# The first upsampling of the MLP: TensorE reads its operand with columns outside

## The chip, the cores and the metric

The kernel runs on one core of a Trainium2 chip, as one program in one launch. The metric is device time in microseconds (us). Three executions before the change took 17002.19, 17007.7 and 17019.74 us; their median is 17007.7 us. The profile is of a further execution.

## The reference, cut to what matters

Eight images of 48 x 48 points with 96 channels pass through four layers, each added to its input behind a group normalisation (`_gn`). Layers 0, 2 and 3 are selective scans and hold nearly all of the work. Layer 1, the MLP, is where the change lies: the normalised image is upsampled along both sides by a band-limited filter, goes through two dense maps with a quadratic between them, and is filtered back to 48 x 48.

```python
x = x + _L0_conv_ref(_gn(x), ...)     # scan in four directions
xc = jnp.transpose(x, (0, 3, 1, 2))   # layer 1
xu = _upsample_rfft(xc)               # height and width
h = jnp.transpose(xu, (0, 2, 3, 1))
h = h @ W1.T + b1
h = coef[:, 0] + coef[:, 1] * h + coef[:, 2] * (h * h)
h = h @ W2.T + b2
hl = _lpf_rfft(jnp.transpose(h, (0, 3, 1, 2)), cutoff=0.5)
out = hl[:, :, ::2, ::2]              # added to x
x = x + _L2_conv_ref(_gn(x), ...)     # scan along lines
x = x + _L3_conv_ref(_gn(x), ...)     # scan in four directions
```

The filters are linear, so the kernel applies each as a matrix: `upt` (48 x 73) takes 48 points to 73, and `downt` (73 x 48) takes them back. An upsampling along the height is thus one matrix product with the height on the partitions.

## The kernel before, in words

**Stages.** The program has three stages one behind another: `ss2d("l0")` (layer 0), `lines` (layer 2) and `ss2d("l3")` (layer 3). Each walks over 8 images, 4 directions and 5 blocks of up to 10 lines of 48 points, 160 blocks in all. A block takes four turns, so a stage has 640 turns and an image 80. A turn is one pass of the loop in `scans`: three scans on VectorE (L337, 128 x 968 values each), the exponentials that feed them on ScalarE (`make_da`, L329, six a turn, written to PSUM tile `ps_da`, which has two buffers), the products that feed them on VectorE and GpSimd (`make_dbu`, L305), the products behind them on GpSimd (`make_hc`, L343) and the sums over states on TensorE (`reduce`, L363 and L365). VectorE waits for `ps_da`; ScalarE in turn waits for the scan that frees a buffer of it.

**The guest.** Layer 1 has no stage of its own. A class `Guest` hands out its steps one by one between the turns' instructions, during the stages `l0` and `lines`, image by image as layer 0 finishes them. Stage `l3` has the same code as `l0` and no guest. The order of every engine's instructions is the order in which the program is written; no scheduler reorders them. `aside`, called twice a turn (for slots `at` and `at + 1`), first calls `guest.settle()`, which issues what had been left behind (the ScalarE half of a step), and last `guest.turn()`, which issues new steps: for a step of kind "psum" the matmul at once, into a free PSUM bank (`side` or `s1` in `l0`, shown as `ps_side` and `ps_s`; `sa` or `sb` in `lines`), and its ScalarE half at the next `settle`, one half turn later. The exponentials of the following half turn are queued on ScalarE right behind what `settle` issued.

**The first upsampling.** For each image, 24 channels at a time are loaded as `xt`, height on the 48 partitions, then channel, then width (L1130). `heighten` (L1144) is called three times for each such load, with 8 channels each: a TensorE matmul of `upt` with 8 channels x 48 columns of `xt` (384 columns in all, L1145) and a ScalarE copy from PSUM into `xh` (L1147), which is laid out as 73 rows of height on partitions, then width, then 24 channels. Both `xt` and `xh` are parts of one tile, `g_room` in the profile. When three copies are done, `keep` (L1160) sends `xh` to memory as `upd`. Before the change the matmul's output runs channel by channel, and the copy turns the order: it reads PSUM straight on and writes each next value 24 values (96 bytes) on. There are 8 x 4 x 3 = 96 such matmuls and 96 such copies in the program. In the profile each matmul of 32-bit values stands as two records, so L1145 has 192.

**Other lines that the steps touch.** `done` in `ss2d` (L762) is a ScalarE copy from PSUM into an image laid out by lines; in two of the four directions it writes by columns, so that each next value is 48 values (192 bytes) on, in the other two straight on. `s0` in `ss2d` (L721) is a TensorE matmul whose moving operand is that same kind of view: straight on in two directions, 192 bytes a step in the two others. The four directions follow each other for each image in the order straight, column, column, straight. `raw` (L711) is a TensorE matmul into bank `s1`, whose result ScalarE reads at L715.

The helper that the copy used before splits a row of PSUM into runs of 48:

```python
def rows(t, n):
    return t[:, :n].rearrange("p (r s) -> p r s", s=SEG)   # SEG = 48
```

Of the kernel before, what the change touches and what calls it, by code (L numbers as in the profile page):

```python
# [15 lines left out]
H, W, C = 48, 48, 96  # L16
# [20 lines left out]
UG = 73  # L37
# [3 lines left out]
HS = 8  # L41
# [21 lines left out]
def rows(t, n):  # L63

    return t[:, :n].rearrange("p (r s) -> p r s", s=SEG)
# [37 lines left out]
def vss_stack_kernel(ctx: ExitStack, tc: tile.TileContext, i: dict, out: bass.AP):  # L103
    nc = tc.nc
# [890 lines left out]
    class Guest:  # L995
# [54 lines left out]
        def items(self):  # L1050
# [4 lines left out]
            upt, downt = self.tile([H, UG], "upt"), self.tile([UG, H], "downt")  # L1055
# [4 lines left out]
            def part(at, rows_, *shape):  # L1060
                n = int(np.prod(shape))
                v = room[:rows_, at:at + n]
                return v.rearrange("p (a b) -> p a b", b=shape[1]) if len(shape) == 2 else v
# [34 lines left out]
            xt, xh = part(0, H, HC, W), part(HC * W, UG, W, HC)  # L1098
# [6 lines left out]
            for b in range(nb):  # L1105
# [36 lines left out]
                       lambda p: nc.scalar.activation(bl, p[:C, :1], AF.Identity, bias=bias))  # L1142

                def heighten(s0):  # L1144
                    return ("psum", lambda p: nc.tensor.matmul(p[:UG, :HS * W], lhsT=upt, rhs=xt[:, s0:s0 + HS, :],  # L1145
                                                               start=True, stop=True),
                            lambda p: nc.scalar.copy(xh[:, :, s0:s0 + HS].rearrange("p w c -> p c w"),  # L1147
                                                     rows(p[:UG], HS * W)))

                for c0 in range(0, C, HC):  # L1150
                    for s0 in range(0, HC, HS):
                        yield heighten(s0)
                    yield "wait", 1
                    if c0 + HC < C:
                        yield "do", lambda: load_xt(c0 + HC)
                    yield "wait", 1

                    def keep():
                        for s in UCUT:
                            nc.sync.dma_start(upd[s, :, c0:c0 + HC], xh[s])  # L1160
                    yield "do", keep
                    yield "wait", 2
# [194 lines left out]
```

## Time and profile before

| | |
|---|---|
| median of three executions | 17007.7 us |
| the profiled execution | 17010.73 us |
| its span, first to last instruction | 17007.9 us |
| mean granted clock of TensorE | 0.854 |
| first scan of `l0`, of `lines`, of `l3` | 103.8, 5844.3, 11616.4 us |
| L337 scans, 5760 | 11822.8 us busy, mean 2075 ns |
| L329 exponentials, 11520 | 7419.0 us busy, mean 649 ns |
| L343 products on GpSimd, 3840 | 10065.4 us busy, mean 2635 ns |
| L1145 matmul records of the first upsampling, 192 | 482 ns the shortest, 915 ns the longest |
| L1147 copies of the first upsampling, 96 | 1092 ns the shortest, 1239 ns the longest |

The first copy starts at 1101.4 us and the last at 8788.6 us, so 72 of the 96 stand in `l0` and 24 in `lines`. "Busy" is the time in which at least one instruction of a group runs; on ScalarE an instruction's record can reach into the next one's, so that the distance between two starts is shorter than the duration. In a windows view, a row gives for a stretch of the span the busy time of each engine with its count of records, the granted clock of TensorE as a share of full speed (PEclk), and what the DMA engines did.

### The profile page before, as it was taken

How to read it: one execution, taken by the hardware profiler on the slowest of the kernel's cores; microseconds unless marked ns; L12 is line 12 of the kernel's file. 1: busy time of each engine (PE TensorE's matmuls, PEld its weight loads, DVE VectorE, ACT ScalarE, POOL GpSimd, SP SyncE). 2: the span in 40 equal slices, each digit the busy share in tenths (PEclk: the TensorE clock that was granted, in tenths of full speed). 3: DMA queues.
4: the chain of work that ended last, by engine and by line, in shares of the span. 5: the costliest groups of instructions: out<-in, count | busy, mean ns of one | idle time of the engine just before them, and what ended most of it. 6: DMA issues, size and time to landing. Idle time of an engine off the chain costs nothing.

```text
span 17007.9 us, 172189 instructions
## 1 busy us (share of the span) xinstructions
PE 13000.3 (76%) x53740; PEld 4643.6 (27%) x53740; DVE 15774.2 (93%) x9680; ACT 13824.5 (81%) x20812; POOL 15185.0 (89%) x7999
## 2 busy tenths in 40 slices
PE   6778887888787777777777777776777777777776
PEld 1223232333332333233323332221222222222221
DVE  7999999999999799999999999997999999999998
ACT  6878878888787688888888888886877878878876
POOL 7998989998889788888888888887999999999998
PEclk7878888889898789889989998887888878878887
DMA  4555555564555444544454444444545455555554
GB/s 149 180 170 172 180 163 182 171 185 169 173 172 179 141 153 167 167 161 164 158 171 159 158 166 160 160 156 139 180 168 181 173 170 176 176 172 176 175 176 143
DMA packets 931143, 2844.03 MB, mean 167 GB/s; under 512 B 396668, under 2 KB 464988, under 8 KB 803406
## 3 DMA queue, kind: packets, MB, share of 16 engines
q1 hardware_dynamic: 930222, 2833.03, 49.9%
q8 instruction: 422, 6.91, 0.2%
q14 instruction: 499, 4.09, 0.1%
HBM read 2384.40 MB, written 448.17 MB: 167 GB/s over the span
## 4 chain that ended last, share of the span: by engine, by line
POOL 24%; DVE 22%; ACT 21%; issue 18%; PE 10%; DMA 3%; SPq 1%; POOLq 0%; DVEq 0%; ACTq 0%
DVE dbu L337 15%; POOL dbu L343 14%; ACT ps_da L329 8%; POOL dbu L305 7%; DVE dbu L305 6%; ACT L329 3%; POOL dds L507 3%; PE ps_y L363 2%; ACT ps_b L286 1%; DMA bc<-bcd 1%; DMA dd<-dds 1%; PE ps_side L582 1%; PE ps_s L711 1%; ACT L739 1%; PE ps_sb L874 1%
## 5 line engine op out<-in xcount | busy, mean ns | idle before, releaser
L337 DVE TENSOR_TENSOR_SCAN dbu<-ps_da,dbu 128x968 f32<-128x968 f32 (+3 forms) x5760 | 11822.8, 2075 | 782.2 <-ACT ps_da L329 644.7
L343 POOL TENSOR_TENSOR dbu<-dbu,bc 128x1440 f32<-128x1440 f32 (+1 forms) x3840 | 10065.4, 2635 | 1486.5 <-DVE dbu L337 948.7
L329 ACT ACTIVATE ps_da<-dd,w_l_a 128x484 f32<-128x484 f32 (+3 forms) x11520 | 7419.0, 649 | 2395.5 <-DVE dbu L337 2166.1
L363 PE MATMUL ps_y<-dbu,w_red 128*32 128x480 f32 (+1 forms) x23040 | 4282.5, 658 | 1806.8 <-POOL dbu L343 1744.4
L365 PE MATMUL ps_y<-dbu,w_red 128*32 128x480 f32 (+1 forms) x7680 | 4242.3, 658 | 0.0
L305 DVE TENSOR_TENSOR dbu<-dd,ps_b 128x962 f32<-128x962 f32 (+5 forms) x2720 | 3810.3, 1401 | 186.2 <-ACT ps_b L286 137.7
L305 POOL TENSOR_TENSOR dbu<-dd,bc 128x481 f32<-128x481 f32 (+3 forms) x2080 | 3883.9, 1883 | 0.0
L363 PEld LDWEIGHTS ps_y<-dbu,w_red 128*32 128x32 f32 x23040 | 708.5, 118 | 5244.5 <-POOL dbu L343 3767.7
L286 ACT COPY ps_b<-bc 128x482 f32<-128x482 f32 (+2 forms) x2560 | 1364.6, 533 | 116.5 <-DVE dbu L305 104.1
L582 PE MATMUL ps_side<-xpad,w_l_cw 128*128 128x480 f32 (+1 forms) x2880 | 1323.1, 597 | 46.7 <-ACT g_room L1183 16.4
L329 ACT ACT_TABLE_LOAD x993 | 1274.0, 1283 | 17.4
L711 PE MATMUL ps_s<-bcl,square 128*128 128x480 f32 (+1 forms) x1280 | 874.3, 773 | 231.3 <-ACT dds L715 82.6
L359 PE MATMUL ps_y<-big,eye 128*128 128x480 f32 (+1 forms) x960 | 745.5, 865 | 254.2 <-ACT big L762 249.7
L721 PE MATMUL ps_s<-big,square 128*128 128x480 f32 (+1 forms) x1280 | 844.5, 790 | 66.4 <-ACT g_room L1183 18.0
L507 POOL TENSOR_TENSOR dds<-dds,big 96x960 f32<-96x960 f32 (+1 forms) x320 | 706.7, 2209 | 123.3 <-ACT dds L739 120.4
L582 PEld LDWEIGHTS ps_side<-xpad,w_l_cw 128*128 128x128 f32 x2880 | 559.8, 205 | 789.3 <-issue 671.9
L874 PE MATMUL ps_sb<-xpad,square 128*128 128x480 f32 (+1 forms) x1280 | 613.6, 626 | 46.9 <-ACT g_room L1183 22.8
L365 PEld LDWEIGHTS ps_y<-dbu,w_red 128*32 128x32 f32 x7680 | 647.5, 117 | 0.0
L874 PE MATMUL ps_sa<-xpad,square 128*128 128x480 f32 (+1 forms) x1280 | 521.3, 548 | 0.0
L917 PE MATMUL ps_sa<-xpad,square 128*128 128x480 f32 (+1 forms) x320 | 251.5, 881 | 342.1 <-ACT g_room L1183 109.7
L762 ACT COPY big<-ps_y 96x480 f32<-96x480 f32 (+1 forms) x640 | 471.7, 737 | 39.0 <-PE ps_y L365 37.6
L711 PEld LDWEIGHTS ps_s<-bcl,square 128*128 128x128 f32 x1280 | 249.6, 239 | 759.5 <-ACT dds L715 327.2
(250 smaller groups left out, 12525.4 us busy)
## 6 DMA issues: line engine op xcount, KB each, us to landing
dd<-dd SPq DMA_DIRECT2D x512, 1452.0 KB
bc<-bcd SPq DMA_DIRECT2D x1536, 480.0 KB
dd<-dd SPq DMA_DIRECT2D x256, 1440.0 KB
dd<-dds SPq DMA_DIRECT2D x1536, 121.0 KB
dd<-dd SPq DMA_DIRECT2D x128, 1164.0 KB
bc<-bcd SPq DMA_DIRECT2D x384, 384.0 KB
dd<-dds SPq DMA_DIRECT2D x768, 120.0 KB
dd<-dd SPq DMA_DIRECT2D x64, 1152.0 KB
```

The costliest lines, as they stand in the source:

```text
L286: nc.scalar.copy(bps[t][:, :bcs[t][0].shape[1]], bcs[t][0])
L305: engine.tensor_mul(o, du, by.unsqueeze(1).to_broadcast([P, hi - lo, by.shape[1]]))
L329: nc.scalar.activation(da[:, at:at + b.m], b.got[half][:, u % 3, 0, :], AF.Exp, scale=a[:, b.k, ci:ci + 1])
L337: nc.vector.tensor_tensor_scan(db, da, db, 0.0, ALU.mult, ALU.add)
L343: nc.gpsimd.tensor_mul(h, h, bcs.pop(2 * t + sub)[1].unsqueeze(1).to_broadcast([P, 3, n]))
L363: nc.tensor.matmul(y[32 * g:32 * g + 32, :n], lhsT=wc["red"][:, :32], rhs=hc[:, g, b.at], start=False, stop=(slot == 3))
L365: nc.tensor.matmul(y[DH:, :n], lhsT=wc["red"][:, 32:], rhs=hc[:, 2, b.at], start=False, stop=(slot == 3))
L507: nc.gpsimd.tensor_mul(du, dt, u)
L582: nc.tensor.matmul(pu[:, :n], lhsT=flat[:, at:at + P], rhs=xpad[:, r0 + dy:r0 + dy + nr, dx:dx + W], start=(tap == 0), stop=(tap == 8))
L711: nc.tensor.matmul(got["p"][:, :n], lhsT=wide("dtw", (2 * b.k + half) * DH), rhs=b.bcl[:, :n], start=True, stop=True)
L721: nc.tensor.matmul(got["p"][:, :n], lhsT=wide("xp", (2 * b.k + half) * NBC), rhs=uall[:, half], start=(half == 0), stop=(half == 1))
L874: nc.tensor.matmul(got["u", half][:, :n], lhsT=wide("cw", at), rhs=shifted(off), start=(tap == 0), stop=(tap == 3))
```

## The change

The matmul of `heighten` is given its moving operand with the two free sides exchanged: width outside, channel inside. Its 384 output columns so come out in the order in which `xh` is laid out, and the copy writes them in runs of 8 values side by side (one run for each of 48 columns, the next run 96 bytes on). PSUM is read straight on, as before. TensorE's reads now go 48 values (192 bytes) on at each step within a run of 8, and then back to the next column. The result in `xh`, the loads of `xt`, the DMAs to `upd` and all later steps are the same. The sequence of instructions is the same on all five engines; what differs is the access pattern of 96 matmuls and 96 copies.

```diff
                 def heighten(s0):
-                    return ("psum", lambda p: nc.tensor.matmul(p[:UG, :HS * W], lhsT=upt, rhs=xt[:, s0:s0 + HS, :],
+                    return ("psum", lambda p: nc.tensor.matmul(p[:UG, :HS * W], lhsT=upt, rhs=xt[:, s0:s0 + HS, :].rearrange("p c w -> p w c"),
                                                                start=True, stop=True),
-                            lambda p: nc.scalar.copy(xh[:, :, s0:s0 + HS].rearrange("p w c -> p c w"),
-                                                     rows(p[:UG], HS * W)))
+                            lambda p: nc.scalar.copy(xh[:, :, s0:s0 + HS],
+                                                     p[:UG, :HS * W].rearrange("p (w c) -> p w c", c=HS)))
```

## Prediction

> **What bounds the kernel now.** I first read the page's busy times and its chain of waits, then VectorE's list of waits.
>
> ```profile
> PE 13000.3 (76%) x53740; PEld 4643.6 (27%) x53740; DVE 15774.2 (93%) x9680; ACT 13824.5 (81%) x20812; POOL 15185.0 (89%) x7999
> POOL 24%; DVE 22%; ACT 21%; issue 18%; PE 10%; DMA 3%; SPq 1%; POOLq 0%; DVEq 0%; ACTq 0%
> ```
>
> ```profile
> DVE dbu L337 <- ACT ps_da L329: 644.7, 674, 4.9
> ```
>
> No engine is alone in charge, but VectorE (DVE) is nearest: it is idle for 17008 - 15774 = 1234 us in all, and for 644.7 us of those (674 waits) it waits for ScalarE's exponentials. So ScalarE's time counts where an exponential is late for a scan, and only there. Every us by which the time can fall here must come out of such waits.
>
> The two groups that the change touches are small. The view of line L1147 gives its copies by PSUM bank with shortest, median and longest duration in ns, and further down how often ScalarE (ACT) stood idle for the matmul just before (us in all, times):
>
> ```profile
> L1147 ACT COPY g_room<-ps_side x49: 1101/1108/1159, 1101.4 to 5548.8; 73x384 f32<-73x384 f32 x49
> ...
> L1147 ACT COPY g_room<-ps_s x23: 1092/1232/1239, 1102.7 to 5518.5; 73x384 f32<-73x384 f32 x23
> ...
>   PE ps_side L1145: 26.9, 22
>   PE ps_s L1145: 4.2, 4
>   PE ps_sb L1145: 3.8, 5
> ```
>
> 96 copies of 1.1 us are 106 us, 0.6% of the span; 31 of them came after ScalarE had waited for their matmul, 34.9 us in all.
>
> **Part 1: the copies become cheaper.** Duration isn't what the engine's queue pays. In the timeline of ScalarE around three copies (start, duration, line), the first starts at 1206.41 and the next instruction at 1207.24:
>
> ```profile
> 1206.41 1.10 ACT L1147 COPY g_room<-ps_side 73x384 f32<-73x384 f32 x1
> 1207.24 1.23 ACT L1147 COPY g_room<-ps_s 73x384 f32<-73x384 f32 x1
> 1208.19 2.73 ACT L329 ACTIVATE ps_da<-dd,w_l_a 128x484 f32<-128x484 f32 x4
> ```
>
> A copy of 1.10 us thus takes 0.83 us of the queue (the one out of `ps_s` 0.95). What it takes afterwards is not in this trace, since no ScalarE instruction writes runs of 8. The nearest rows are the copies of L762, also PSUM to SBUF and also 384 values: first one that writes 192 bytes on at each value, then one that writes straight on.
>
> ```profile
> 447.42 0.82 ACT L762 COPY big<-ps_y 96x384 f32<-96x384 f32 x1
> 448.04 0.60 ACT L726 COPY bcl<-ps_s 38x480 f32<-38x480 f32 x1
> ...
> 289.72 0.47 ACT L762 COPY big<-ps_y 96x384 f32<-96x384 f32 x1
> 290.09 0.55 ACT L726 COPY bcl<-ps_s 38x480 f32<-38x480 f32 x1
> ```
>
> They take 0.62 and 0.37 us of the queue. I take 0.37, because seven of eight values lie beside the one before; the ends are 0.37 and 0.83 (no gain), with 0.62 between. That the copy grows dearer I exclude: no side of it steps further than it does today. So ScalarE is relieved of 96 x (0.83 - 0.37) = 44 us, by the middle row of 96 x 0.21 = 20 us, at worst of nothing.
>
> [...]
>
> **Part 2: the matmuls become dearer.** TensorE's operand is now read 192 bytes on at each value. L721 does the same reading in two of its directions. Windows with two of its 384-column matmuls each at full clock, straight and by columns, and then around one of each at half clock (busy us, records, PEld, granted clock):
>
> ```profile
> 1223.00:1229.00 6.00, 1.45 (x4) 0.76 (x4) 1.00 0.19 42
> 1044.00:1050.00 6.00, 2.82 (x4) 0.71 (x4) 1.00 0.13 50
> 2254.60:2256.33 1.73, 1.67 (x3) 1.07 (x4) 0.50 0.88 209
> 2445.40:2447.17 1.77, 1.67 (x3) 1.03 (x4) 0.50 0.99 319
> ```
>
> At full clock a matmul goes from 1.45/2 = 0.72 to 2.82/2 = 1.41 us, +0.69. At half clock both take 1.67: the slow clock hides the reading. In the timeline, 64 of the 96 L1145 matmuls take under 1.2 us (0.86 mostly, clock 1.0) and 32 take 1.4 to 1.55 (clock 0.5). So TensorE gains 64 x 0.69 = 44 us of work. The ends are 0 (if the short runs of 8 reuse something) and, if a pass costs what a copy of today takes for 384 values, 2 x 0.83 - 0.72 = 0.94 us each, 60 us. I take 44, the row with the same distance in bytes.
>
> [...]
>
> So about the same time leaves ScalarE as enters TensorE. Which of them is worth more?
>
> **What ScalarE's time is worth.** In the burst above VectorE ran like this (idle time and what ended it in brackets):
>
> ```profile
> 1206.03 2.17 DVE L337 TENSOR_TENSOR_SCAN dbu<-ps_da,dbu 128x968 f32<-128x968 f32 x1 [0.53 <-ACT ps_da L329]
> ...
> 1209.66 4.24 DVE L337 TENSOR_TENSOR_SCAN dbu<-ps_da,dbu 128x968 f32<-128x968 f32 x2 [0.42 <-ACT ps_da L329]
> ```
>
> The two copies pushed the exponential at 1208.19 back, and the scan waited 0.42 us for it. A gain of 0.92 us there is worth 0.42. I followed all 96 copies in the timeline, from each copy along ScalarE until either an exponential that a scan waits for, or an idle time of ScalarE's own, which swallows the gain. 59 copies come to a scan's wait; these are 45 waits of 40.7 us together. Capping each by 0.455 us for every copy ahead of it leaves **21 us**. The other 37 copies gain nothing that I can see. Once a scan starts earlier, what is late next is GpSimd (89% busy) and the next exponential, which already lie behind that scan; I let the gain stand.
>
> **What TensorE's time costs.** 33 copies start right at the end of their matmul (the 31 waits, and two shorter). 14 of these matmuls ran at full clock, and 8 of the 14 lead to a scan's wait. There the copy starts 0.69 later and takes 0.46 less of the queue: the 0.46 counted above goes, and 0.23 comes on top, 8 x 0.69 = 5.5 us. The other matmuls end up to 5 us ahead of their copy, mostly over 0.7, so the half turn between them covers it; if that cover went, it would be the rest of the 44 us.
>
> A second reading of both prices: windows over images 2 to 6 of stage `l0`, and the same images of `l3`, which has no guest (sums):
>
> ```profile
> sum 3557.60, PE 2916.22 PEld 1175.43 DVE 3266.82 ACT 2947.44 POOL 3195.34; mean PE 583.24 PEld 235.09 DVE 653.36 ACT 589.49 POOL 639.07
> sum 3344.90, PE 2481.13 PEld 751.15 DVE 3243.86 ACT 2700.51 POOL 3184.97; mean PE 496.23 PEld 150.23 DVE 648.77 ACT 540.10 POOL 636.99
> ```
>
> The guest adds 246.9 us of ScalarE and 435.1 us of TensorE, and the stretch grows by 212.7 us. If ScalarE alone is to blame, each of its us costs 0.86; if TensorE alone, 0.49. With 21/44 = 0.48 for ScalarE, TensorE's is left with (212.7 - 0.48 x 246.9) / 435.1 = 0.22, and its 44 us cost 9.5 us. That is the upper of two values, 5.5 the lower; I take 6.
>
> **Nothing else moves.** Order and number of instructions are the same on every engine, and weight loads, DMAs and `xh` are unchanged; SP's and GpSimd's queues see only the shifted times.
>
> **Sum.** -21 + 6 = -15 us on a profiled execution of 17010.7 us (span 17007.9), which is 3 us over the median of the runs shown. From the median of 17007.7 I come to **16993 us**, 0.09% less. A measurement of this kernel can tell about 0.2%, or 34 us, from no change.
>
> **The rivals.**
> - *All of ScalarE's relief is on the path* (0.22). At 0.86 to 1 us for each us, 44 us become 38 to 44, and the time 16964 to 16970. For it: the first reading of the `l0` and `l3` sums, and that I followed each copy only to the first scan. Against it: 37 copies run into an idle time of ScalarE.
> - *The wait moves to the matmul* (0.13). If most matmuls run at full clock now and more copies stand right behind theirs, the copy starts 0.69 later and ends when it does today: -5 to +5 us, 17003 to 17013. The same time comes out if the runs of 8 don't help the copy and TensorE's cover holds, so that the change does not do what it says. For it: 31 copies wait already. Against it: 19 of the 33 were at half clock.
> - *Slower: TensorE's queue is what the guest's work costs* (0.15). The longer matmul stands ahead of `raw` (L711) and `reduce` (L363), whose results ScalarE and GpSimd's buffers wait for. At 0.49 us for each us the 44 cost 21.5 us, at 1 all of 44: 17029 to 17052. It decides once a us of TensorE costs more than one of ScalarE, which by the two sums is at 212.7 / (246.9 + 435.1) = 0.31. Against it: TensorE is 76% busy, and VectorE's waits name ScalarE far more than TensorE.
>
> My forecast, -30 to -5 us, has 0.50. Faster by over 0.2% is the first rival, 0.22; slower by over 0.2% is half of the last one, 0.08; 0.70 lies within. The range goes from 16965 (44 us, the bound of the copy's gain) to 17026 (towards the slower rival's first price).
>
> **What would show it.** Right: L1147 near 0.47 us with starts 0.37 apart; a full-clock L1145 pair near 1.4 us and a half-clock one still at 1.55; VectorE's 644.7 us of waits for `ps_da` down by about 15; ScalarE's 34.9 us of waits for L1145 up by some 10. Wrong: copies that stay above 0.8 us; L1145 pairs unchanged, or near 1.7; waits of VectorE or ScalarE for TensorE that grow by tens of us; or a fall of the waits for `ps_da` by over 30 us.

## The result and the profile after

| | before | after |
|---|---|---|
| median of 12 runs each, us | 16995.58 | 16963.53 |
| ratio, 95% interval | | 0.9979, 0.9971 to 0.9987 |
| both kernels a second time (`after_again`), us | 17001.36 | 16962.68 |
| ratio, 95% interval | | 0.9978, 0.9970 to 0.9987 |
| profiled execution, us | 17010.73 | 16961.89 |
| span of it, us | 17007.9 | 16959.3 |

The change is worth 32 to 39 us by the medians and 22 to 49 us by the first interval. The forecast was 15 us, from 17007.7 to 16993. Nine more runs of before put its median 12 us lower, and the time after is 1.5 us under the low end of the range. The direction was right and the prices of the two edits nearly so; the gain is about twice what was forecast.

Page of after, busy times and shares of the chain that ended last, and VectorE's wait for the exponentials (644.7 before):

```profile
PE 13019.0 (77%) x53740; PEld 4652.3 (27%) x53740; DVE 15770.0 (93%) x9680; ACT 13783.3 (81%) x20812; POOL 15183.9 (90%) x7999
POOL 27%; DVE 21%; ACT 20%; issue 17%; PE 11%; DMA 3%; SPq 1%; POOLq 0%; DVEq 0%; ACTq 0%
```

```profile
DVE dbu L337 <- ACT ps_da L329: 617.7, 646, 4.5
```

ScalarE is 41 us less busy than in the profile of before, TensorE 19 us busier, and VectorE waits 27 us less for exponentials. The two changed groups in after, copies first (shortest, median, longest in ns, and ScalarE's waits for the matmul), then matmul records:

```profile
L1147 ACT COPY g_room<-ps_side x49: 467/473/518, 1104.4 to 5509.1; 73x384 f32<-73x384 f32 x49
...
L1147 ACT COPY g_room<-ps_s x23: 460/473/476, 1105.7 to 5480.0; 73x384 f32<-73x384 f32 x23
...
  PE ps_side L1145: 26.3, 23
  PE ps_s L1145: 11.1, 9
  PE ps_sb L1145: 6.2, 8
```

```profile
L1145 PE MATMUL ps_side<-g_room,g_upt x98: 820/834/914, 1102.8 to 5506.4; 48*73 48x384 f32 x98
...
L1145 PE MATMUL ps_s<-g_room,g_upt x46: 820/820/914, 1104.2 to 5478.4; 48*73 48x384 f32 x46
```

The copies take 0.473 us for 1.108, as the straight L762 row of before had it. The matmul records take 0.82 at least for 0.482; the longest stay at 0.915, as at half clock nothing changes (1.55 us a matmul in both). From the start of a matmul's first record to the end of its second, most full-clock matmuls of L1145 take 1.49 us for 0.86, and all 96 together 144 us for 104: 40 us more, where 44 were forecast. (The 19 us by which TensorE is busier on the page count all of its work, and with it what the clock did elsewhere.) What was off by more is what these prices are worth.

### The profile page after: what moved, and what is told of

Read it like the earlier page. It is cut to its first block, busy times and chain, and to the rows that moved or that the text cites. A ratio compares the mean times of both kernels' runs of the same rounds, so it can differ in the third digit from the quotient of the medians.

```text
span 16959.3 us, 172189 instructions
## 1 busy us (share of the span) xinstructions
PE 13019.0 (77%) x53740; PEld 4652.3 (27%) x53740; DVE 15770.0 (93%) x9680; ACT 13783.3 (81%) x20812; POOL 15183.9 (90%) x7999
## 4 chain that ended last, share of the span: by engine, by line
POOL 27%; DVE 21%; ACT 20%; issue 17%; PE 11%; DMA 3%; SPq 1%; POOLq 0%; DVEq 0%; ACTq 0%
POOL dbu L343 16%; DVE dbu L337 13%; POOL dbu L305 7%; ACT ps_da L329 7%; DVE dbu L305 5%; ACT L329 3%; POOL dds L507 3%; PE ps_y L363 2%; DMA bc<-bcd 1%; ACT ps_b L286 1%; DMA dd<-dds 1%; PE ps_side L582 1%; PE ps_s L711 1%; PE ps_sb L874 1%; PE ps_sa L893 1%
## 5 line engine op out<-in xcount | busy, mean ns | idle before, releaser
L337 DVE TENSOR_TENSOR_SCAN dbu<-ps_da,dbu 128x968 f32<-128x968 f32 (+3 forms) x5760 | 11825.6, 2076 | 745.3 <-ACT ps_da L329 617.7
L711 PE MATMUL ps_s<-bcl,square 128*128 128x480 f32 (+1 forms) x1280 | 868.4, 769 | 220.6 <-ACT dds L715 93.8
L359 PE MATMUL ps_y<-big,eye 128*128 128x480 f32 (+1 forms) x960 | 744.4, 864 | 248.7 <-ACT big L762 244.0
L721 PE MATMUL ps_s<-big,square 128*128 128x480 f32 (+1 forms) x1280 | 845.4, 791 | 60.9 <-ACT g_room L1183 18.5
L762 ACT COPY big<-ps_y 96x480 f32<-96x480 f32 (+1 forms) x640 | 472.4, 738 | 38.9 <-PE ps_y L365 38.3
L711 PEld LDWEIGHTS ps_s<-bcl,square 128*128 128x128 f32 x1280 | 249.7, 239 | 743.5 <-ACT dds L715 306.5
```

The source lines that it names most:

```text
L337: nc.vector.tensor_tensor_scan(db, da, db, 0.0, ALU.mult, ALU.add)
L711: nc.tensor.matmul(got["p"][:, :n], lhsT=wide("dtw", (2 * b.k + half) * DH), rhs=b.bcl[:, :n], start=True, stop=True)
L721: nc.tensor.matmul(got["p"][:, :n], lhsT=wide("xp", (2 * b.k + half) * NBC), rhs=uall[:, half], start=(half == 0), stop=(half == 1))
```

## The experiments

**How they are read.** A turn's length is the distance between the first L337 scans of two turns in the timeline; the last turn reaches to the end of the span. Five profiles of the kernel before agree in the turns that hold a copy (56 of the 1920) to within 2 us in sum, so these turns can be compared one by one. Each row below is a profile's sum against the mean of those five, in us.

| kernel | 12 turns, 3 copies | 16 turns, 2 copies | 28 turns, 1 copy | all 56 | the other turns |
|---|---|---|---|---|---|
| before, five profiles | -1.3 to 1.2 | -0.9 to 0.8 | -1.1 to 0.5 | -1.8 to 2.0 | -8.3 to 12.7 |
| after, four profiles | -17.7 to -17.2 | -6.9 to -5.5 | -1.3 to 0.4 | -24.2 to -23.5 | -17.7 to -7.2 |
| copy_only | -17.3 | -10.5 | -2.6 | -30.5 | -4.8 |
| matmul_only | 1.2 | 5.0 | 2.7 | 9.0 | 0.1 |
| psum_turns | -17.5 | -11.2 | -2.6 | -31.3 | -2.8 |
| copy_twice | 37.8 | 34.8 | 14.7 | 87.2 | 7.0 |
| matmul_twice | 19.1 | 13.1 | 7.1 | 39.2 | 2.5 |
| copy_first / second / third | -7.0 / -6.1 / -5.2 | -5.9 / -2.7 / -1.5 | -2.1 / -0.2 / -3.8 | -15.0 / -9.1 / -10.5 | 18.0 / -8.8 / 1.9 |

**copy_only: the copy without the matmul.**

```diff
-  lambda p: nc.scalar.copy(xh[:, :, s0:s0 + HS].rearrange("p w c -> p c w"), rows(p[:UG], HS * W))
+  lambda p: nc.scalar.copy(xh[:, :, s0:s0 + HS], p[:UG, :HS * W].rearrange("p (w c) -> p w c", c=HS))
```

> The kernel before with the new copy alone: the matmul reads straight on as before, the copy reads and writes in the new order, so the values of this step land in the wrong places of xh. ScalarE is relieved of 96 x 0.46 = 44 us of queue and TensorE pays nothing. Theory 'all on the path' (each us of ScalarE worth 0.86 to 1): 38 to 44 us faster, ratio near 0.9976. Theory 'as counted' (0.48): 21 us faster, ratio near 0.9988. Theory 'TensorE carries the guest's cost': no change, ratio 1.000.

Measured: 16963.17 against 16997.39 us, ratio 0.9981 (0.9972 to 0.9989), 34 us faster, or 0.78 us for each us of the queue; 30.5 us (0.69) in the turns with copies. That lies between the first two theories, and the interval (19 to 48 us) holds both. The turns separate them: -17.3 where the forecast's count credits 9.5 (turns with three copies), -10.5 where it credits 7.6, -2.6 where it credits 4.0.

**matmul_only: the matmul without the copy.**

```diff
-  rhs=xt[:, s0:s0 + HS, :],
+  rhs=xt[:, s0:s0 + HS, :].rearrange("p c w -> p w c"),
```

> The kernel before with the new reading of the matmul alone: the copy is the old one, so the values of this step land in the wrong places of xh. The matmuls cost 42 to 44 us more of TensorE. 'All on the path' for ScalarE: 0 to 5 us slower, ratio 1.000. 'As counted': 6 to 10 us slower, ratio near 1.0005. 'TensorE carries the cost': 21 us slower, ratio near 1.0013.

Measured: 17007.52 against 16997.39, ratio 1.0007 (0.9998 to 1.0016); 9.0 us in the turns with copies. This is the forecast's 6 to 10. Beside the new copy the price is 30.5 - 24.0 = 6.5 us. In nine of the twelve turns with three copies it is nothing (five of these take 8.78 us without and with it). In eight of the nine the first two matmuls end over 2 us ahead of their copies in before, and the third runs at half clock.

**before_again, before_third: how much is chance.** The kernel before, unchanged.

> The kernel before, unchanged, for a second profile of it: ratio 1.000. It tells how much of the 24 us that the turns around the copies lost between the two profiles, and of the 27 us that the turns between them lost, is the difference of two executions. If the loss around the copies is the change's and the rest is chance, the spans around the copies stay as in the first profile of before to within a few us, and the rest shifts by 10 us or more.

> The kernel before once more, for a third profile: the turns with copies as in the first two to within 3 us in sum; the other turns differ by 5 to 20 us from either, if what they lost in the changed kernel's two profiles (11 and 13 us against the second profile of before, 27 and 29 against the first) can be chance. If they lie within 5 us of the first profile of before, the second was the odd one, and the loss outside the turns with copies is the change's.

Measured: 17001.86 against 16997.39, ratio 1.0003 (0.9994 to 1.0011), and 16998.58 against 16998.6. The turns with copies are the same; the other turns differ by up to 18 us between these three profiles of one kernel. One of these turns shows what differs. The columns are the stretch, its length, busy time and records of PE, PEld, DVE, ACT and POOL, granted clock, DMA share and GB/s; first before, then before_again:

```profile
2353.60:2367.00 13.40, 13.17 (x51) 7.87 (x52) 8.69 (x7) 9.14 (x14) 9.94 (x9) 0.62 0.30 86
```

```profile
2349.90:2359.50 9.60, 8.91 (x56) 5.46 (x56) 8.74 (x7) 8.84 (x14) 9.60 (x6) 1.00 0.41 134
```

VectorE and ScalarE do the same work; TensorE's clock was 0.62 in the one and 1.00 in the other, and the turn took 3.8 us more. TensorE is busy for 13.17 of the 13.40 us of the longer one, so there it sets the length. Over 17 profiles (all kernels of this study but done_turned), turns of `l0` and `lines` without copies are over 1 us off their median 356 times, and in 292 of these the longer side has the lower clock. That the two go together doesn't tell which comes first in each of them. In the clock records of the trace of before the granted clock is 0.5 or 1.0, and 1393 of the 1394 spells of one value last a whole multiple of 3.413 us. That the same work meets another clock from run to run, the turns above show (0.62 and 1.00). What makes the clock fall was not shown: in the 3.413 us ahead of its 697 falls TensorE was busy for 0.40 of the time in the median.

**copy_twice and matmul_twice: larger doses.** Each old copy, or each old matmul, is issued twice.

```diff
-  lambda p: nc.scalar.copy(xh[...], rows(p[:UG], HS * W))
+  lambda p: [nc.scalar.copy(xh[...], rows(p[:UG], HS * W)) for _ in range(2)]
```

> The kernel before with each of the 96 old copies issued twice (the second writes the same again): 96 x 0.83 = 80 us more of ScalarE's queue. One price for all of ScalarE's time, as copy_only has it (34 us for 44, 0.78): 62 us slower, ratio near 1.0037. 'As counted': 59 copies lead straight to a scan's wait and now cost all of their 0.83, 49 us; the other 37 first fill the idle time behind them, so 49 to 60 us, ratio 1.0029 to 1.0035. If ScalarE's time is not what counts: no change.

Measured: 17088.81 against 17001.36, ratio 1.0051 (1.0038 to 1.0065), 87 us slower. The dose was larger than expected. ScalarE in copy_twice, a pair of copies and what follows:

```profile
1214.88 2.24 ACT L1147 COPY g_room<-ps_side 73x384 f32<-73x384 f32 x2
1216.85 2.38 ACT L1147 COPY g_room<-ps_s 73x384 f32<-73x384 f32 x2
```

A pair takes 1216.85 - 1214.88 = 1.97 us of the queue where one took 0.83: the second, which writes the same place, starts 0.03 us after the first has ended. So 96 x 1.14 = 109 us were added, and 87 us are 0.80 for each. ScalarE's time is worth 0.7 to 0.8 in these places, in both directions.

> The kernel before with each of the 96 matmuls issued twice: 64 x 0.81 + 32 x 1.55 = 101 us more of TensorE and nothing more of ScalarE. At the price of the forecast (0.12 to 0.22 for each us): 12 to 22 us slower, ratio 1.0007 to 1.0013. At the price 0.49 of the slower rival: 50 us slower, ratio 1.0029. If TensorE's time is free: 1.000.

Measured: 17035.6 against 17001.36, ratio 1.0022 (1.0013 to 1.0031), 34 us slower, and 39 us in the turns with copies. Here the dose was smaller than expected: from first start to last end the L1145 matmuls take 185 us for 104, 81 us more and not 101. The price is thus 0.42 for each us by the medians and 0.48 in the turns, against 0.22 in matmul_only (9.0 for 40 us), so TensorE's time has no single price here. What matmul_only leaves as it is, the matmuls at half clock, is doubled here, and 19 of the 33 copies that start right at the end of their matmul in before wait for one of these. In the turn that the next paragraphs follow, the third copy waits 2.37 us for its matmul in place of 1.09, and the turn is 1.29 us longer. The twelve turns with three copies make up 19.1 of the 39.2 us.

**copy_first, copy_second, copy_third: which copy gives what.** The new copy for one of each three channel groups alone, for example

```diff
+  lambda p: nc.scalar.copy(xh[:, :, s0:s0 + HS], p[:UG, :HS * W].rearrange("p (w c) -> p w c", c=HS))
+  if s0 == 8 else nc.scalar.copy(xh[:, :, s0:s0 + HS].rearrange("p w c -> p c w"), rows(p[:UG], HS * W))
```

> The kernel before with the new copy for the second of each three alone (channels 8 to 15, 32 copies; in the turns with three copies it is the one out of bank s1), so those values land in the wrong places of xh. Read in the turn that begins at 1205.0 us in before (8.78 us long; 7.29 with all three copies new). 'Chain through TensorE' (this copy frees the bank for L711, behind which the third matmul of L1145 stands, behind which the third copy waits): its 0.76 us of latency (1.23 to 0.47) all come back, the turn is 0.76 shorter. 'Count to the first scan': the scan's wait of 0.42 goes and ScalarE's idle time of 1.09 swallows the rest, the turn is 0.42 shorter.

> The same with the new copy for the first of each three alone (channels 0 to 7). Both theories: the turn at 1205.0 us is 0.42 to 0.46 shorter, the 0.46 by which the copies behind it start earlier.

> The same with the new copy for the third of each three alone (channels 16 to 23). Both theories: the turn at 1205.0 us is 0.46 shorter, since the scan behind it waits 0.90. L711's waits for L1147 stay as in before. If the three gains add up (0.46 + 0.76 + 0.46 = 1.68) to what all three gave (1.49), the chain carries all of it but what a scan did not wait for.

The turn that these name by its start at 1205.0 us starts at 1206.03 in the profile of before and at 1205.05 in that of before_again. Measured in that turn (8.78 us): 8.20 with the first, 8.15 with the second, 8.31 with the third new; the gains are 0.58, 0.63 and 0.47 and sum to 1.68. TensorE in before at this turn, then TensorE and VectorE in copy_second:

```profile
1204.11 0.80 PE L1145 MATMUL ps_s<-g_room,g_upt 48*73 48x384 f32 x2
1208.52 1.97 PE L711 MATMUL ps_s<-bcl,square 128*128 128x480 f32 x2 [3.61 <-ACT g_room L1147]
1210.42 1.55 PE L1145 MATMUL ps_side<-g_room,g_upt 48*73 48x384 f32 x2
```

```profile
1205.78 1.97 PE L711 MATMUL ps_s<-bcl,square 128*128 128x480 f32 x2 [3.01 <-ACT g_room L1147]
1207.67 1.55 PE L1145 MATMUL ps_side<-g_room,g_upt 48*73 48x384 f32 x2
```

```profile
1203.91 2.17 DVE L337 TENSOR_TENSOR_SCAN dbu<-ps_da,dbu 128x968 f32<-128x968 f32 x1 [0.54 <-ACT ps_da L329]
...
1212.06 2.17 DVE L337 TENSOR_TENSOR_SCAN dbu<-ps_da,dbu 128x968 f32<-128x968 f32 x1 [0.78 <-ACT ps_da L329]
```

In before the turn's first scan starts at 1206.03, so L711 stands 1208.52 - 1206.03 = 2.49 us behind it; with the second copy new it is 1205.78 - 1203.91 = 1.87, 0.62 earlier. The matmul behind L711, the third copy behind that and the next turn's scan all come 0.63 earlier. The gain went through TensorE, not into ScalarE's idle time: 0.63 was measured where the count to the first scan has 0.42. It is less than the 0.76 expected, because the new copy takes 0.60 behind an old one and not 0.47. The first copy gave more than expected for the mirrored reason: the old copy behind it takes less of the queue (0.82 us for 0.95). The third gave what both theories say.

**psum_turns: PSUM is written in steps.** The matmul reads straight on and its output is turned.

```diff
-  nc.tensor.matmul(p[:UG, :HS * W], lhsT=upt, rhs=xt[:, s0:s0 + HS, :].rearrange("p c w -> p w c"),
+  nc.tensor.matmul(p[:UG, :HS * W].rearrange("p (w c) -> p c w", c=HS), lhsT=upt, rhs=xt[:, s0:s0 + HS, :],
```

> The same result another way: the matmul reads straight on, as before, and writes PSUM in the new order (each next column 8 values, 32 bytes, on), and the copy is the new one. No row of the traces shows a matmul that writes PSUM in steps. [...] If writing in steps is free, the records are 0.48 us at full clock, the copies 0.47, and the time is that of copy_only: as low as after or up to 10 us lower.

Measured: 16968.84 against 16997.39, ratio 0.9983 (0.9974 to 0.9991). The matmul records, 482 ns at least and 915 at most as in before:

```profile
L1145 PE MATMUL ps_side<-g_room,g_upt x98: 482/584/915, 1100.4 to 5513.9; 48*73 48x384 f32 x98
...
L1145 PE MATMUL ps_s<-g_room,g_upt x46: 482/483/914, 1101.1 to 5485.0; 48*73 48x384 f32 x46
```

Writing these 32-bit outputs in 32-byte steps costs nothing here: the shortest records take 482 ns as in before, where the stepped read of after has 820. The turns with copies are as in copy_only, 7 us under after; in the medians that isn't seen, since the intervals of psum_turns and after overlap.

**done_turned: the same in the larger group.** With the edit of psum_turns in it. `b.nr` is the number of lines of a block, 10 or 8.

```diff
-  nc.tensor.matmul(y[32 * g:32 * g + 32, :n], lhsT=wc["red"][:, :32], rhs=hc[:, g, b.at], ...)
+  nc.tensor.matmul(y[32 * g:32 * g + 32, :n].rearrange("p (s r) -> p r s", r=b.nr), lhsT=wc["red"][:, :32],
+                   rhs=hc[:, g, b.at].rearrange("p (r s) -> p r s", s=SEG), ...)   # column directions
-  nc.scalar.copy(so_far(b, half)[:DH], rows(y[:DH], b.n))
+  nc.scalar.copy(v.rearrange("p r s -> p s r"), y[:DH, :b.n].rearrange("p (s r) -> p s r", r=b.nr))
-  return eye, so_far(b, half)                       # what L359 reads; v is so_far(b, half)
+  return eye, v.rearrange("p r s -> p s r")          # column directions
```

> psum_turns carried to the larger group of the same kind: in the two column directions of both scan stages of layers 0 and 3, the matmuls that sum over states write PSUM in image order (40-byte steps), so that done's copy (L762) and the matmul that reads the running sum (L359) work on runs of 10 values side by side. 256 copies of 480 values go from 0.775 to 0.451 us of queue and 64 of 384 from 0.617 to 0.371: 99 us less of ScalarE; 320 matmuls of L359 lose about 0.7 us each at full clock. If writing PSUM in 40-byte steps stays free for summing matmuls, as it was in psum_turns at 32: 40 to 80 us faster than psum_turns, ratio to before 0.993 to 0.996. If summing in steps costs what a stepped read costs (0.82 for 0.48 a record), some 13000 records get dearer and the kernel is slower than before by over 2%.

Measured: 16950.73 against 17001.36, ratio 0.9971 (0.9960 to 0.9983), the fastest of all kernels here, though its interval overlaps that of after. The copies (turned ones are L772 here), and the summing matmuls (mean ns of one; 684 in before):

```profile
L772 ACT COPY big<-ps_y x320: 465/551/560, 307.0 to 16739.0; 96x480 f32<-96x480 f32 x128, 96x384 f32<-96x384 f32 x32
```

```profile
L370 PE MATMUL ps_y<-dbu,w_red 128*32 128x480 f32 x18432 | 3586.2, 682 | 1734.0 <-POOL dbu L343 1706.1 <-POOL dbu L314 21.2
```

Both came as hoped: the copies are at the straight price (551 ns in the median, 547 in L774, the straight ones here) and summing in 40-byte steps is free. (The means of 684 and 682 take in all records of the line, of which a third are turned; over both lines that sum these are 10240 records, not 13000. In the turns of the column directions, but for a few at either end, it is 721 here and 716 in psum_turns, with a median of 566 in both.) TensorE was relieved too, as L359 now reads runs of 10 or 8 values and no longer 192 bytes on at each value; before, then done_turned:

```profile
L359 PE MATMUL ps_y<-big,eye x960: 483/968/1169, 290.2 to 16975.3; 128*128 128x480 f32 x160, 128*128 128x384 f32 x32
```

```profile
L359 PE MATMUL ps_y<-big,eye x960: 483/565/1170, 291.4 to 16919.2; 128*128 128x480 f32 x160, 128*128 128x384 f32 x32
```

The 640 records concerned take 189 us less in sum than in psum_turns. Yet the two reliefs together gave some 22 us more than psum_turns gave (51 against 29), where 40 to 80 were expected. That is 0.2 for each of the 99 us of ScalarE, if the relief of L359 is worth nothing, and less if it is worth something. VectorE's wait for exponentials is 611.5 us here and 614.7 in psum_turns, and ScalarE's wait for scans rose from 2196.5 to 2216.9. That fits copies that stood where no scan was waiting, so that ScalarE waits instead.

**after_again, before_fourth, before_fifth, after_third, after_fourth: is the rest the change's?**

> The changed kernel once more, unchanged. If the 20 us that the turns around the copies lost against the second profile of before are the change's own, they are there again to within 5 us, and what the turns between the copies lose or gain differs from the first profile by up to 10 us either way. Ratio near 0.998 if all that was measured is the change; near 0.9988 if the forecast's 15 to 21 us are and the rest was chance.

> The kernel before, a fourth profile. If the rest is chance, the other turns lie anywhere from 20 us under to 20 over the mean of the first three, and so do those of the changed kernel. If the change has a part in it, the four or five profiles of before stay apart from those of the changed kernel, which keep 10 to 25 us under the mean. The turns with copies stay within 3 us of the first three.

> The changed kernel, a third profile. The turns with copies 22 to 24 us under before. Other turns: by chance anywhere from 20 under to 20 over the mean of before; by the change 10 to 25 under it.

> The kernel before, a fifth profile; the same is expected of it as of the fourth, in the turns with copies and in the others.

> The changed kernel, a fourth profile; the same is expected of it as of the third, in the turns with copies and in the others.

Measured: after_again 16962.68 against 17001.36 us (0.9978, 0.9970 to 0.9987); before_fourth and before_fifth 16990.52 and 17001.51, after_third and after_fourth 16966.2 and 16966.6, beside 16995.46 of before. The turns with copies are 23.5 to 24.2 us shorter in all four profiles of after. Its other turns are -13.3, -17.7, -7.2 and -7.4, mean -11.4; those of before 12.7, -5.8, 0.2, -8.3 and 1.3. The two sets overlap (-8.3 in before, -7.2 in after). Their means differ by 11.4 us with a standard error of 4.4.

## Why the forecast was half of the gain

**The prices of the two edits: nearly right.** The copy takes 0.37 of the queue, as forecast. The matmul was sized by two L721 matmuls back to back (0.72 and 1.41 us each); those of L1145 stand alone, and most go from 0.86 to 1.49 us at full clock, +0.63 for +0.69. At half clock nothing changes, as forecast (1.55 us in both).

**TensorE's cost of 6 us: right.** It is 6.5 us beside the new copy and 9.0 alone. The slower rival, at 21.5 us or more, is ruled out for this dose by matmul_only's turns; its interval alone, up to 27 us, would not do it.

**ScalarE's relief of 21 us: too small, and this is the step that failed.** It was 30.5 us in the turns with copies. The prediction followed each copy "until either an exponential that a scan waits for, or an idle time of ScalarE's own, which swallows the gain", and stopped there. Of the 0.92 us freed ahead of the scan at 1209.66 us it kept the scan's own wait, 0.42. The rest it left out, as by its rule the next idle time of ScalarE would swallow it. That idle time was not slack. In before it stands ahead of the third copy and is 1.09 us long, and the next turn's scan then waits 0.90 us:

```profile
1212.01 1.11 ACT L1147 COPY g_room<-ps_side 73x384 f32<-73x384 f32 x1 [1.09 <-PE ps_side L1145]
```

```profile
1214.80 2.17 DVE L337 TENSOR_TENSOR_SCAN dbu<-ps_da,dbu 128x968 f32<-128x968 f32 x1 [0.90 <-ACT ps_da L329]
```

The idle time ends with the third matmul, that matmul stands behind L711 on TensorE, and L711 waits 3.61 us for the second copy to free its bank. So the rest of the relief came round through TensorE to the third copy and the scan behind it. In after, in the same turn, ScalarE and VectorE:

```profile
1205.42 0.47 ACT L1147 COPY g_room<-ps_side 73x384 f32<-73x384 f32 x1
1205.79 0.47 ACT L1147 COPY g_room<-ps_s 73x384 f32<-73x384 f32 x1
1206.16 2.66 ACT L329 ACTIVATE ps_da<-dd,w_l_a 128x484 f32<-128x484 f32 x4
1209.80 0.47 ACT L1147 COPY g_room<-ps_side 73x384 f32<-73x384 f32 x1 [0.98 <-PE ps_side L1145]
```

```profile
1207.12 1.13 DVE L305 TENSOR_TENSOR dbu<-dd,ps_b 128x962 f32<-128x962 f32 x1
1208.17 6.30 DVE L337 TENSOR_TENSOR_SCAN dbu<-ps_da,dbu 128x968 f32<-128x968 f32 x3
```

ScalarE's idle time ahead of the third copy is still there (0.98 for 1.09), although the copies before it end 1.2 us earlier; both ends of it moved. Both waits of VectorE, 0.42 and 0.90 us, are gone, and three scans run back to back. The turn is 8.78 - 7.29 = 1.49 us shorter; the count gave it 0.42 + 0.455 = 0.87.

Eight of the twelve turns with three copies run like this one. In each of them the new copy in first place alone gives 0.58 or 0.59 us, in second place 0.63 or 0.64, in third place 0.46 to 0.48, and copy_only gives 1.50 or 1.69. Together the eight gain 12.6 us in copy_only where the count has 7.0, which is 5.6 of the 9.4 us by which the relief was too small. In 24 other turns every copy runs into an idle time of ScalarE, in 19 of them one that a scan ends, and there the count's nothing was right: copy_only is 3 us longer in them, and no gain shows. The 24 turns that are left gain 21.1 us for 14.2; what carried the gain there was not followed.

**The sum.** In the turns with copies it is -24 us, where -15 was forecast. The medians show 32 to 39, and the other turns carry the rest, 11 us in the mean of four profiles. Where those turns differ by over 1 us from one profile to the next, the longer one mostly has the lower clock (292 of 356 times in 17 profiles). Whether the change itself moves them its way is not settled: the two sets of profiles overlap, and the ratio's interval (22 to 49 us) holds the 24 alone. The timed runs lean towards yes, for the means of before and after differ by 35 us in the first set and 37 in the second, with standard errors of 3.7 and 2.1. psum_turns, with the same copies, leans towards no, with 30 us by its runs and -2.8 in its other turns. No run shows a mechanism for those 11 us.

That the time itself came out 29.5 us under the forecast of 16993 is in part chance in its base: 12 us are the lower median of before, 17 the larger gain. The low end of the range, 16965, stands for 44 us in the prediction, but 17007.7 - 44 is 16963.7; the measured 16963.53 lies 0.2 us under that.

**The rivals.** "All of ScalarE's relief is on the path" gave the nearest time (16964 to 16970), helped by the lower base; its price, 0.86 to 1 for each us, was measured as 0.69 in the turns and 0.78 over the run. "The wait moves to the matmul" did not come: ScalarE's waits for L1145 rose from 34.9 to 43.6 us (31 to 40 waits), about the 10 us that the forecast named.

## What to carry to other kernels

An idle time on the relieved engine swallows a gain only if what ends it does not itself hang on that engine: follow its releaser one queue further before a gain is written off. What time on an engine is worth depends on the place and the dose, 0.7 to 0.8 for these copies, 0.2 or less for those of L762, and 0.2 to 0.5 for the matmuls of one line, so count it from the waits in that stretch. Executions of this one kernel differ by 10 to 20 us, mostly in turns where the granted clock differs too; compare the same turns in several profiles before a cause is named. When a dose is added, measure it in the trace before a price is worked out: both doses here were not what was expected.

## What was not expected of the hardware

A matmul that writes PSUM in steps of 32 or 40 bytes is as fast as one that writes straight on (482 ns at least in psum_turns and in before for 384 columns; for 480, in the column directions, a median of 566 ns in done_turned and in psum_turns), while reading its moving operand in 192-byte steps takes 0.82 for 0.48 us a record at full clock (L1145 in after and before). Reading it in runs of 10 values (8 in the shorter blocks) with jumps between the runs is free again: the median of L359's 960 records from `big` falls from 968 ns in before to 565 in done_turned, beside 564 for the 640 that read `ub` straight on. So the turn of an order was free in one place of three: 0.46 us a copy on ScalarE's write, 0.63 us a matmul on TensorE's read, nothing on its write to PSUM. A ScalarE copy that writes 96 bytes on at each value (0.83 us of the queue for 384 values, L1147 in before) is slower than one that writes 192 bytes on (0.62, L762 in before).
